# The last stage of a two-layer decoder: three results of a token side by side, read by half batches, one batch added by TensorE

## The chip, the cores and the metric

The kernel runs on one core of one Trainium2 chip. The metric is the device time of one execution in microseconds (us); three runs of the kernel before gave 1203.73, 1205.29 and 1206.92 us, a median of 1205.29. Everything below about where time goes comes from one further execution that was recorded by the hardware profiler.

## The reference, cut to what matters

The network has two layers, each an attention to a context and then a mixture of experts, with residual sums. Only the last mixture matters here: 2048 tokens of 256 numbers, 15 experts of which each token uses 3, and a shared expert that every token uses.

```python
def _L1_ffn_ref(x, gate_w, fc1_w, fc1_b, geglu_mult, fc2_w, fc2_b, s_fc1_w, ...):
    ...
    scores = jax.nn.softmax(xt @ gate_w.T, axis=-1)
    topk_w, topk_idx = jax.lax.top_k(scores, TOPK)              # TOPK = 3 of E = 15
    topk_w = topk_w / (jnp.sum(topk_w, axis=-1, keepdims=True) + 1e-20)
    ...
    a = jax.nn.gelu(g, approximate=False) * xh * geglu_mult[:, None, :]
    yexp = jnp.einsum('etf,edf->etd', a, fc2_w) + fc2_b[:, None, :]
    y = jnp.einsum('etd,te->td', yexp, comb)
    ...
    ys = as_ @ s_fc2_w.T + s_fc2_b
    return (y + ys).reshape(s, b, d)
...
x = x + _L1_ffn_ref(_layernorm(x, axis=-1), ...)
```

## The kernel before, in words

The 2048 tokens are 4 batches of 512. A batch lies in SBUF as one tile `x[b]` of 128 partitions x 4 x 256 numbers (token `k * 128 + p` of the batch in partition `p`, place `k`), 4 KB in each partition. `x[b]` holds the running residual sum all through the kernel and is written to the output at the end.

In the last mixture each token is copied three times, once for each expert that it chose, into a DRAM table ordered by expert (`xs`). With a copy go its weight and the row of the result table `y1` (3 x 2048 rows of 1 KB, in DRAM) into which its result shall be put. This row number is made once by `numbers` (L508): `token1` at L525 gives choice `k` of token `t` the row `k * 2048 + t`, so a batch's results lie in three places of 512 rows each.

The routed experts run by pairs of 128-row tiles in `pipeline` (L469, called near the end of the kernel): `fetch1` loads rows and weights, `turn1` transposes, `hidden1` makes the hidden values (TensorE, ScalarE, VectorE), and `output1` multiplies by the second weights, scales on ScalarE (L1366) and scatters 128 rows to `y1` by an indirect DMA from GpSimd (L1368). These scatters are collected in the list `adds`. Some of the pairs run only if the number of pairs calls for it.

The shared expert has two halves of 256 hidden numbers. `shared_expert(b, new)` (L1179) is a generator: for each half it makes two hidden tiles (L1188 on TensorE, L1194 on ScalarE, and on VectorE the gate in L1174 and L1177), giving way twice for each tile; then for each of the batch's four token tiles it sums four products in PSUM (L1203) and adds the sum to `x[b]` on VectorE (L1207). For batches 0 to 2 all of it is done before the routed experts. For batch 3, `last`, only the first half's hidden tiles are made ahead (four steps of the generator); the rest is left for the end, where it keeps TensorE in work while the scatters land.

The tail, after the pipeline, is this:

- `last` is run to its end (L1405).
- For each batch, in the order 0 to 3, and for each choice `k`, 512 rows of `y1` are read into a tile `yr1` (L1411, by SP's queue, 4 pieces of 1 KB for each partition) and added to `x[b]` in one VectorE instruction of 128x1024 (L1413). The tag `yr1` has 3 buffers. Every read waits for all scatters in `adds`.
- After a batch's three additions `x[b]` is written to the output (L1414), 512 KB in one DMA.

Here the order of the instructions on the engines is chosen by a scheduler. In the rest of the last mixture it is the order of the program's text (`tc.manual_schedule`). In the order that the scheduler chose for the tail, VectorE takes the additions of batch 0 and the first of batch 1 in turn with the two remaining gates of `last`; the four L1207 additions stand after batch 1's second addition. On SP the reads of batch 0 and the first two of batch 1 come first, and an output follows when its additions are done, with the next reads behind it.

Of the kernel before, what the change touches and what calls it, by code (L numbers as in the profile page):

```python
# [12 lines left out]
F32 = mybir.dt.float32  # L13
# [3 lines left out]
ALU = mybir.AluOpType  # L17
AX = mybir.AxisListType
ENG = mybir.EngineType
# [3 lines left out]
P = 128  # L23
B, S, D = 4, 512, 256
T = B * S
NT = T // P
TB = S // P
# [16 lines left out]
PAIR = 2 * P  # L44
# [17 lines left out]
E1, K1, F1 = 15, 3, 256  # L62
E1S = E1 + 2
FC = F1 // P
# [11 lines left out]
def decoder_kernel(ctx: ExitStack, tc: tile.TileContext, a: dict, out: bass.AP):  # L76
    nc = tc.nc
# [5 lines left out]
    def after(ins, earlier, reason):  # L83
        for e in earlier:
            tc.add_manual_dep(
                ins, e.name,
                mybir.DependencyInfo(mybir.DependencyClass.Sync, mybir.DependencyReason.DATA),
                reason=reason,
            )


    x = [const.tile([P, TB, D], F32, name=f"x{b}") for b in range(B)]
# [37 lines left out]
    ident = const.tile([P, P], F32, name="ident")  # L130
# [2 lines left out]
    make_upper_triangular(nc, upper, 1.0, diag=False)  # L133
    ones = const.tile([P, P], F32, name="ones")
    nc.gpsimd.memset(ones, 1.0)


    slots = dram.tile([SLOTS + E0 * T, ROW], F32, name="slots")
    y0 = dram.tile([K0 * T, D], F32, name="y0")
    xs = dram.tile([E1 * T + 2 * PAIR, ROW], F32, name="xs")  # L140
    y1 = dram.tile([K1 * T, D], F32, name="y1")
# [366 lines left out]
    def numbers():  # L508


        def ramp(name, shape, pattern, base=0):
            t = const.tile([P, *shape], F32, name=name)
            nc.gpsimd.iota(t, pattern=pattern, base=base, channel_multiplier=0, allow_small_or_imprecise_dtypes=True)
            return t

        named = ramp("named", (E1,), [[1, E1]])
        slot0 = ramp("slot0", (E0,), [[REGION0, E0]])
        drop0 = ramp("drop0", (E0,), [[T - REGION0, E0]], SLOTS)  # L520
        token0 = const.tile([P, NT, K0], I32, name="token0")
        nc.gpsimd.iota(token0, pattern=[[P, NT], [T, K0]], base=0, channel_multiplier=1)
        slot1 = ramp("slot1", (E1,), [[T, E1]])
        token1 = const.tile([P, NT, K1], I32, name="token1")
        nc.gpsimd.iota(token1, pattern=[[P, NT], [T, K1]], base=0, channel_multiplier=1)  # L525

        def choices(t, n, k):
            return t[:, :n].unsqueeze(1).unsqueeze(1).to_broadcast([P, TB, k, n])

        def tiles(t, n):  # L530
            return t.unsqueeze(1).to_broadcast([P, TB, n])

        index = const.tile([P, 1], F32, name="index")
        nc.gpsimd.iota(index, pattern=[[0, 1]], base=0, channel_multiplier=1, allow_small_or_imprecise_dtypes=True)
        twice = const.tile([P, 1], F32, name="twice")
        nc.gpsimd.iota(twice, pattern=[[0, 1]], base=0, channel_multiplier=2, allow_small_or_imprecise_dtypes=True)
        some0 = ramp("some0", (TILES0,), [[P, TILES0]])
        full0 = const.tile([P, len(FULL0)], F32, name="full0")  # L540
        for i, v in enumerate(FULL0):
            nc.gpsimd.memset(full0[:, i : i + 1], float(v))
        base0 = ramp("base0", (E0,), [[TILES0, E0]], -E0 * TILES0)
        some1 = ramp("some1", (PAIRS1 - 1,), [[PAIR, PAIRS1 - 1]], PAIR)
        base1 = ramp("base1", (E1,), [[PAIRS1, E1]], 1 - E1 * PAIRS1)
        earlier = const.tile([P, E1, E1], F32, name="earlier")
        nc.gpsimd.memset(earlier, 1.0)
        nc.gpsimd.affine_select(
            out=earlier, in_=earlier, compare_op=ALU.is_gt, fill=0.0,
            base=0, pattern=[[1, E1], [-1, E1]], channel_multiplier=0,  # L550
        )
        ffn0.number(choices(named, E0, K0), tiles(slot0, E0), token0, base0)
        ffn1.number(choices(named, E1, K1), tiles(slot1, E1), token1, base1)
        ffn0.drop, ffn0.some, ffn0.full, ffn1.some = tiles(drop0, E0), some0, full0, some1
        return index, named, earlier, twice
# [381 lines left out]
    def begin0(b):  # L937
        if b == 0:
            lists.extend(numbers())
        return iter(())  # L940
# [164 lines left out]
    with ExitStack() as first:  # L1105
# [5 lines left out]
        new = dict(  # L1111
            pt=lambda: ps_t.tile([P, DC, P], F32, name="prt", tag="prt"),
            pg=lambda: ps_h.tile([P, PAIR], F32, name="pg", tag="pg"),
            pu=lambda: ps_h.tile([P, PAIR], F32, name="pu", tag="pu"),
            py=lambda: ps_y.tile([P, D], F32, name="py", tag="py"),
            rT=lambda: mw.tile([P, DC, P], F32, name="rT0", tag="rT0"),
            hT=lambda: mw.tile([P, NF // 2, PAIR], F32, name="hT", tag="hT"),
            sg=lambda: mw.tile([P, PAIR], F32, name="sg", tag="sg"),
            ysb=lambda: mw.tile([P, D], F32, name="ysb", tag="ysb", bufs=6),
# [52 lines left out]
    def gate(o, pv, b1, f, gl):  # L1172

        nc.vector.tensor_scalar(  # L1174
            o, pv, b1[:, f : f + 1], b1[:, 2 * FC + f : 2 * FC + f + 1], ALU.add, ALU.mult
        )
        nc.vector.tensor_tensor(o, o, gl, ALU.mult)  # L1177

    def shared_expert(b, new):  # L1179

        aTs = []
        for w1, w2, b1 in both:
            aT = new["aT"]()
            for f in range(FC):
                pg, pv = new["p"](), new["p"]()
                for ph, col in ((pg, F1 + f * P), (pv, f * P)):
                    for c in range(DC):
                        nc.tensor.matmul(  # L1188
                            ph, w1[:, c, col : col + P], ffn1.xT[b][:, c, :],
                            start=(c == 0), stop=(c == DC - 1),  # L1190
                        )
                    if ph is pg:
                        gl = new["gl"]()
                        nc.scalar.activation(gl, pg, AF.Gelu, bias=b1[:, FC + f : FC + f + 1])  # L1194
                        yield PEP
                gate(aT[f], pv, b1, f, gl)
                yield PEP
            aTs.append((aT, w2))
        for k in range(TB):
            py = new["p"]()[:, :D]  # L1200
            for i, (aT, w2) in enumerate(aTs):
                for f in range(FC):
                    nc.tensor.matmul(  # L1203
                        py, aT[f][:, k * P : (k + 1) * P], w2[:, f, :],
                        start=(i == 0 and f == 0), stop=(i == 1 and f == FC - 1),
                    )
            nc.vector.tensor_tensor(x[b][:, k, :], py, x[b][:, k, :], ALU.add)  # L1207
            yield PEP

# [88 lines left out]
    mp = m1.enter_context(tc.tile_pool(name="m1p", bufs=1))  # L1298
# [54 lines left out]
    adds = []  # L1353

    def output1(p):
# [24 lines left out]
    new = dict(  # L1380
        p=lambda: ps1.tile([P, S], F32, name="p", tag=next(turns)),
        gl=lambda: mp.tile([P, S], F32, name="gl", tag="gl", bufs=2),
        aT=lambda: [mp.tile([P, S], F32, name="aTs", tag="aTs", bufs=4) for _ in range(FC)],
    )
    turns = itertools.cycle(("pg", "pv", "py"))

    with tc.manual_schedule(engines={ENG.PE, ENG.DVE, ENG.Activation, ENG.SP}):
        for p in range(3):
            fetch1(p)
        for b in more:  # L1390
            for step in (shared_expert, biases) if b < B - 1 else (biases,):
                for _ in step(b, new):
                    pass
        last = shared_expert(B - 1, new)
        for _ in range(4):
            next(last)

# [4 lines left out]
    )  # L1402


    for _ in last:  # L1405
        pass
    for b in range(B):
        for k in range(K1):
            yr = mp.tile([P, TB, D], F32, name="yr1", tag="yr1", bufs=3)
            r = k * T + b * S  # L1410
            read = nc.sync.dma_start(yr, y1[r : r + S, :].rearrange("(k p) d -> p k d", p=P))  # L1411
            after(read.ins, adds, "all results")
            nc.vector.tensor_tensor(x[b], x[b], yr, ALU.add)  # L1413
        nc.sync.dma_start(out[b], x[b])  # L1414
    m1.close()


# [101 lines left out]
```

## Time and profile before

| | |
|---|---|
| median of three runs | 1205.29 us (1203.73 to 1206.92) |
| the profiled execution | 1215.69 us |
| its span | 1214.0 us |
| TensorE busy in the span | 1149.4 us (95%) |
| VectorE, ScalarE, GpSimd busy | 620.4, 459.5, 186.5 us |
| mean granted TensorE clock | 0.955 |
| from 1179.0 us to the end: TensorE, VectorE busy of 35.0 us | 10.36, 18.32 us |
| the same stretch: mean granted clock, DMA share, rate | 0.67, 0.73, 240 GB/s |
| from 1000 to 1160 us: TensorE busy | 158.42 of 160.00 us |

The span runs from the first to the last event of the recorded execution; the profiled execution's own time is 1.69 us longer. The profile lists for each instruction its engine, the line of the kernel, the tiles that it writes and reads, its start and its duration, and, in brackets, how long the engine was idle before it and what ended this idle time. PE is TensorE, DVE is VectorE, ACT is ScalarE, POOL is GpSimd, SP the engine that issues most DMAs. The granted clock is the share of full speed that TensorE was given.

### The profile page before, as it was taken

Reading aid. Unit: us, or ns where it says so; the run is one execution under the profiler, and the core shown is the slowest. Engines: PE = TensorE matmul, PEld = TensorE weight load, DVE = VectorE, ACT = ScalarE, POOL = GpSimd, SP = SyncE. Lnnn points to the kernel's source line nnn. Section 1 sums busy time; section 2 is a strip of 40 time slices with the busy share of each in tenths; the row PEclk is TensorE's granted clock in tenths of the full one; section 3 lists DMA queues with packets and bytes.
Section 4 is the critical chain, followed back from the end, with each engine's and each line's share of the span. In section 5 each row is a group of like instructions: output and inputs, shape, how many; then the busy total and the mean of one; then the engine's idle time right before and its main releaser. Section 6 shows DMA issues by size and latency. Waiting matters only on the chain.

```text
span 1214.0 us, 18265 instructions
## 1 busy us (share of the span) xinstructions
PE 1149.4 (95%) x6582; PEld 738.3 (61%) x6582; DVE 620.4 (51%) x1591; ACT 459.5 (38%) x877; POOL 186.5 (15%) x274
## 2 busy tenths in 40 slices
PE   6999997999999999999999999999999999999982
PEld 3334432788999999997433333433336558888862
DVE  6677773531111111114768688867636435444426
ACT  3365464421222222223266576575653102333320
POOL 2000112042000000002000000211322402333330
PEclk7899998999999999999699999999989989999996
DMA  8999107227788888863101000001100135777737
GB/s 321 406 403 403 69 27 264 75 92 292 302 306 326 316 312 305 317 253 106 35 1 36 1 1 1 27 27 36 44 25 28 53 114 160 218 236 214 226 122 244
DMA packets 64405, 204.73 MB, mean 169 GB/s; under 512 B 9502, under 2 KB 31922, under 8 KB 57392
## 3 DMA queue, kind: packets, MB, share of 16 engines
q1 hardware_dynamic: 56144, 182.93, 42.3%
q0 software_dynamic: 8160, 20.52, 4.6%
q8 instruction: 55, 0.90, 0.3%
q14 instruction: 46, 0.38, 0.1%
HBM read 138.57 MB, written 66.70 MB: 169 GB/s over the span
## 4 chain that ended last, share of the span: by engine, by line
PE 44%; DMA 5%; DVE 4%; issue 1%; ACT 0%; POOL 0%; SPq 0%; DVEq 0%; POOLq 0%
PE sc L696 10%; PE av L735 5%; PE shared L1188 4%; PE pg L1307 3%; PE pv L1307 3%; PE pyp L1361 3%; PE sct L720 3%; DMA y<-ysb,rows 2%; DMA yr<-y 2%; PE pp L673 2%; DVE negmax L701 2%; PE shared L1203 1%; PE po L792 1%; PE pa L645 1%; PE pa L673 1%
## 5 line engine op out<-in xcount | busy, mean ns | idle before, releaser
L701 DVE TENSOR_REDUCE negmax<-sc 128x1 f32<-128x512 f32 x384 | 245.6, 683 | 67.8 <-PE sct L720 59.2
L725 ACT ACTIVATE es<-sct 128x512 f32<-128x512 f32 x384 | 208.5, 596 | 155.2 <-PE sct L720 143.6
L696 PE MATMUL sc<-kT,qT 32*128 32x512 f32 x768 | 255.5, 680 | 5.2 <-DVE negmax L701 2.8
L720 PE MATMUL sct<-qa,kT 32*128 32x512 f32 x768 | 254.3, 660 | 1.7 <-DVE qa L711 1.7
L696 PEld LDWEIGHTS sc<-kT,qT 32*128 32x128 f32 x768 | 82.6, 194 | 103.8 <-DVE negmax L701 59.8
L1015 DVE TENSOR_TENSOR hT<-pu,sg 128x256 f32<-128x256 f32 x96 | 40.8, 425 | 136.5 <-PE pu L1006 131.6
L735 PE MATMUL av<-es,v 128*32 128x512 f32 x768 | 107.2, 619 | 0.1
L1006 PE MATMUL pg<-rT,w 128*128 128x128 f32 x768 | 101.5, 275 | 0.1
L1006 PE MATMUL pu<-rT,w 128*128 128x128 f32 x768 | 101.4, 275 | 0.0
L720 PEld LDWEIGHTS sct<-qa,kT 32*128 32x128 f32 x768 | 78.9, 188 | 26.6 <-issue 16.7
L1006 PEld LDWEIGHTS pg<-rT,w 128*128 128x128 f32 x768 | 93.5, 192 | 0.4 <-issue 0.3
L1006 PEld LDWEIGHTS pu<-rT,w 128*128 128x128 f32 x768 | 93.5, 192 | 0.0
L1024 PE MATMUL py<-w,hT 128*128 128x256 f32 x384 | 86.7, 379 | 0.0
L1368 POOL DMA_INDIRECT y<-ysb,rows x60 | 59.0, 984 | 155.1 <-ACT ysb L1366 143.5
L1024 PEld LDWEIGHTS py<-w,hT 128*128 128x128 f32 x384 | 71.2, 190 | 8.7
L1011 ACT ACTIVATE sg<-pg 128x256 f32<-128x256 f32 x96 | 36.8, 383 | 101.5 <-PE pg L1006 100.5
L378 POOL COPY rows<-weight 128x2 f32<-128x2 f32 (+1 forms) x28 | 4.2, 205 | 434.5 <-DVE weight L341 258.6
L735 PEld LDWEIGHTS av<-es,v 128*32 128x32 f32 x768 | 16.0, 109 | 76.7 <-issue 70.6
L1307 PE MATMUL pg<-rTp,wp 128*128 128x256 f32 x240 | 61.8, 380 | 0.6 <-DVE rTp L1345 0.6
L1307 PE MATMUL pv<-rTp,wp 128*128 128x256 f32 x240 | 61.6, 379 | 0.0
L1030 POOL DMA_INDIRECT y<-ysb,rows x24 | 23.6, 982 | 238.7 <-ACT ysb L1028 236.3
L1174 DVE TENSOR_SCALAR aTp<-pv,wp 128x256 f32<-128x256 f32 x60 | 32.6, 544 | 51.4 <-PE pv L1307 48.3
(257 smaller groups left out, 1490.3 us busy)
## 6 DMA issues: line engine op xcount, KB each, us to landing
w<-in_W12T_dram SPq DMA_DIRECT2D x27, 2048.0 KB
xs<-empty SPq DMA_DIRECT2D x61, 516.0 KB
w<-in_W3T_dram SPq DMA_DIRECT2D x27, 1024.0 KB
wp<-in_w1p_dram SPq DMA_DIRECT2D x30, 515.0 KB
yr<-y SPq DMA_DIRECT2D x20, 512.0 KB
rows<-xs SPq DMA_DIRECT2D x30, 258.0 KB
wp<-in_fc2T_dram SPq DMA_DIRECT2D x30, 256.0 KB
slots<-empty SPq DMA_DIRECT2D x11, 516.0 KB
```

The lines of the kernel that those rows point to most:

```text
L696: nc.tensor.matmul(sc, q[u][32 * j : 32 * j + 32, qt * P : (qt + 1) * P], k[u][32 * j : 32 * j + 32, :], start=True, stop=True,)
L701: nc.vector.tensor_reduce(heads[:, qt, j, HELP[s] : HELP[s] + 1], sc, AX.X, ALU.max, negate=True)
L720: nc.tensor.matmul(sc, k[u][32 * j : 32 * j + 32, kt * P : (kt + 1) * P], qa[u][32 * j : 32 * j + 32, :], start=True, stop=True,)
L725: nc.scalar.activation(t, sc, AF.Exp, scale=p["scale"])
L735: nc.tensor.matmul(av[b, g][32 * j : 32 * j + 32, :], vs[b % NV][:, kt, h : h + 32], es[u, kt, j], start=(first and kt == 0), stop=(last a ...
L1006: nc.tensor.matmul(ph[:, i * n : (i + 1) * n], w[:, c, col + i * P : col + (i + 1) * P], rT[:, c, :], start=(c == 0), stop=(c == DC - 1),)
L1011: nc.scalar.activation(sg, pg, AF.Silu)
L1015: nc.vector.tensor_tensor(h, pu, sg, ALU.mult)
L1024: nc.tensor.matmul(py, hT[f][:, i * P : (i + 1) * P], w[:, f, :], start=(f == 0), stop=(f == NF - 1))
L1188: nc.tensor.matmul(ph, w1[:, c, col : col + P], ffn1.xT[b][:, c, :], start=(c == 0), stop=(c == DC - 1),)
L1307: nc.tensor.matmul(ph[:, :n], w1[:, c, col : col + P], rhs[:, c, :], start=(c == 0), stop=(c == DC - 1),)
L1368: ins = nc.gpsimd.indirect_dma_start(out=y1, out_offset=bass.IndirectOffsetOnAxis(ap=rows[:, i, D : D + 1].bitcast(I32), axis=0), in_=ysb[ ...
```

## The change

The row of a result becomes `3 * t + k`, so that a token's three results lie side by side, 3 KB together. The tail reads them by half batches (256 tokens, 786,432 bytes, 2 pieces of 3 KB for each partition), 8 reads in all, each into a buffer of its own (`bufs=2 * B`). The order of the tail on TensorE, VectorE, ScalarE and SP is given by the program's text. All reads are issued first: batch 0, batch 3, then batches 1 and 2. Then `last` takes the four steps of its second half. Then the batches follow in the same order: batches 0, 1 and 2 by half batches, with three VectorE additions of 128x512 and a store of 256 KB for each half; batch 3 by finishing `last`, in which TensorE adds a token tile's three results to the sum of the shared expert in PSUM, by products with the identity matrix, and VectorE adds this sum to `x[3]`. Batch 3 is stored in one DMA of 512 KB.

On VectorE this order is: the two gates, batch 0's six additions, batch 3's four, batch 1's six, batch 2's six. On TensorE each of the four token tiles of batch 3 has seven instructions in a row: four products of the shared expert and three of the identity. On SP the eight reads stand ahead of all seven stores.

```diff
@@ numbers @@
-        nc.gpsimd.iota(token1, pattern=[[P, NT], [T, K1]], base=0, channel_multiplier=1)
+        nc.gpsimd.iota(token1, pattern=[[P * K1, NT], [1, K1]], base=0, channel_multiplier=K1)
@@ shared_expert @@
-    def shared_expert(b, new):
+    def shared_expert(b, new, results=None):
...
-                        start=(i == 0 and f == 0), stop=(i == 1 and f == FC - 1),
+                        start=(i == 0 and f == 0), stop=(results is None and i == 1 and f == FC - 1),
                     )
+            if results:
+                for c in range(K1):
+                    nc.tensor.matmul(py, ident, results(k, c), start=False, stop=(c == K1 - 1))
             nc.vector.tensor_tensor(x[b][:, k, :], py, x[b][:, k, :], ALU.add)
             yield PEP
@@ decoder_kernel @@
-        last = shared_expert(B - 1, new)
+        found = {}
+        last = shared_expert(B - 1, new, lambda k, c: found[B - 1, k // 2][:, k % 2, c * D : (c + 1) * D])
         for _ in range(4):
             next(last)
...
-    for _ in last:
-        pass
-    for b in range(B):
-        for k in range(K1):
-            yr = mp.tile([P, TB, D], F32, name="yr1", tag="yr1", bufs=3)
-            r = k * T + b * S
-            read = nc.sync.dma_start(yr, y1[r : r + S, :].rearrange("(k p) d -> p k d", p=P))
-            after(read.ins, adds, "all results")
-            nc.vector.tensor_tensor(x[b], x[b], yr, ALU.add)
-        nc.sync.dma_start(out[b], x[b])
+    with tc.manual_schedule(engines={ENG.PE, ENG.DVE, ENG.Activation, ENG.SP}):
+        for b in (0, B - 1, *range(1, B - 1)):
+            for h in range(2):
+                found[b, h] = mp.tile([P, 2, K1 * D], F32, name="yr1", tag="yr1", bufs=2 * B)
+                r = (b * S + h * PAIR) * K1
+                src = y1[r : r + PAIR * K1, :].rearrange("(k p c) d -> p k (c d)", p=P, c=K1)
+                after(nc.sync.dma_start(found[b, h], src).ins, adds, "all results")
+        for _ in range(4):
+            next(last)
+        for b in (0, B - 1, *range(1, B - 1)):
+            if b == B - 1:
+                for _ in last:
+                    pass
+                nc.sync.dma_start(out[b], x[b])
+                continue
+            for h in range(2):
+                xs = x[b][:, 2 * h : 2 * h + 2, :]
+                for c in range(K1):
+                    nc.vector.tensor_tensor(xs, xs, found[b, h][:, :, c * D : (c + 1) * D], ALU.add)
+                nc.sync.dma_start(out[b][:, 2 * h : 2 * h + 2, :], xs)
```

## The prediction

> **What bounds the kernel now.** I read the page's chain of waits first. Its shares say that TensorE sets most of the span, but the change touches only what comes after the routed experts, so the shares say little here. I then asked for the timeline of the last 60 us.
>
> ```profile
> 1174.82 0.98 POOL L1368 DMA_INDIRECT y<-ysb,rows  x1 [0.30 <-issue]
> ...
> 1179.06 8.45 SPq L1411 DMA_DIRECT2D yr<-y  x5
> ...
> 1180.45 1.03 PE L1203 MATMUL p<-ctxT,aTs 128*128 128x256 f32 x4
> ...
> 1184.05 1.22 DVE L1413 TENSOR_TENSOR x<-x,yr 128x1024 f32<-128x1024 f32 x1 [14.50 <-DMA yr<-y]
> 1185.19 0.80 DVE L1174 TENSOR_SCALAR aTs<-p,ctxT 128x512 f32<-128x512 f32 x1
> ...
> 1187.79 7.88 PE L1203 MATMUL p<-ctxT,aTs 128*128 128x256 f32 x28 [6.31 <-DVE aTs L1177]
> ...
> 1197.89 1.23 DVE L1413 TENSOR_TENSOR x<-x,yr 128x1024 f32<-128x1024 f32 x1 [0.23 <-DMA yr<-y]
> 1201.93 1.23 DVE L1413 TENSOR_TENSOR x<-x,yr 128x1024 f32<-128x1024 f32 x1 [2.82 <-DMA yr<-y]
> ...
> 1208.42 1.23 DVE L1413 TENSOR_TENSOR x<-x,yr 128x1024 f32<-128x1024 f32 x1 [2.37 <-DMA yr<-y]
> 1209.68 0.35 SPq L1414 DMA_DIRECT2D out_dram<-x  x1
> ```
>
> The last scatter of results is issued at 1174.82 and has landed by 1179.06, when SP may read them. What follows is a tail of 35 us. VectorE adds each read as it lands and is short of reads: the last waits of 2.82 and 2.37 us end with a landing. The chain of waits agrees: from 1179.5 on it is four stretches of "DMA yr<-y" of 6.81, 5.53, 5.22 and 4.74 us with an addition after each. A read cannot be issued before one of three buffers is free. The windows show that this, and not the DMA engines, holds the reads back.
>
> ```profile
> 1182.50:1183.50 1.00, 0.00 (x0) 0.00 (x0) 0.00 (x0) 0.00 (x0) 0.00 (x0) 1.00 1.06 374
> ...
> 1185.50:1186.00 0.50, 0.00 (x0) 0.00 (x0) 0.50 (x2) 0.00 (x0) 0.00 (x0) 0.50 0.18 61
> 1186.00:1190.50 4.50, 2.71 (x6) 2.19 (x7) 4.50 (x5) 0.00 (x0) 0.00 (x0) 0.50 0.73 235
> ...
> 1191.00:1191.50 0.50, 0.50 (x4) 0.45 (x3) 0.32 (x1) 0.00 (x0) 0.00 (x0) 1.00 1.06 248
> ```
>
> The last three columns are TensorE's granted clock, the DMA engines' share and GB/s. While the first three reads (1.57 MB) move, the rate is 374 GB/s; when all three buffers are full it falls to 61. The clock column matters too: TensorE idled 6.31 us, its clock fell to 0.50, and it was back at 1.00 by 1191.0, 3.2 us after work began again at 1187.79.
>
> **The reads.** The scatter's rows change place in DRAM but stay 1 KB rows, 60 scatters as before (984 ns each on POOL); I cost that at nothing, and the end at 1179.06 stays. There are now 8 reads of 786,432 B in place of 12 of 524,288 B: the same 6.29 MB, each with a buffer of its own, so SP issues them one after another at 0.36 to 0.50 us each, all before any output. A row is now 3 KB. Rows of 1 KB moved at 373 GB/s (above); the first loads, rows of 4 KB, at 406 to 418:
>
> ```profile
> 9.00:11.00 2.00, 1.69 (x5) 0.61 (x3) 0.55 (x3) 1.58 (x3) 0.00 (x0) 1.00 1.02 406
> ```
>
> I take 406, the nearer row, and keep 373 as the other bound. One read is then 0.786/406 = 1.94 us (2.11). The first read of now was issued at 1179.06 and released VectorE at 1184.05: 4.99 us, of which its bytes at 373 are 1.41 and 3.58 is fixed. So the first new read lands at 1179.06 + 3.58 + 1.94 = 1184.6 and the following ones 1.94 us apart: batch 0 at 1184.6 and 1186.5, batch 3 at 1188.5 and 1190.4, batches 1 and 2 at 1192.3, 1194.3, 1196.2 and 1198.2. Now the last one lands at 1208.4. By the reads alone some 10 us are gained.
>
> The Trainium skill has a rule against cutting transfers up: in "DMA: Bandwidth & Descriptors", section "Measured (HBM→SBUF, 128 partitions, SWDGE, issued from GpSimd)", one is to batch to at least 1 MiB, and "Anatomy of one DMA" gives about 2.0 us + bytes/436 GB/s for each. If each read paid that alone, eight would take 8 x 3.8 = 30.4 us and the last would land at 1209.5, with the end 1 to 2 us later than now. The windows above speak against it: queued reads ran without a gap at 374 GB/s.
>
> **Batch 3 on TensorE.** VectorE now makes the gates (L1174, L1177) without an addition ahead of them: the last matmul before them ends at 1180.45, and 0.80 + 0.11 + 0.69 us later, at about 1182.1, all four hidden halves are there (now 1191.3). TensorE runs the fourth product of token tile 0 and then waits in order for batch 3's first read at 1188.5; behind it stand 3 additions by identity and 7 instructions of tile 1 (4 products, 3 additions), then 14 for tiles 2 and 3, 24 in all, 12 of them new. At full clock one is 0.216 us apart from the next (L1361's 16 in 3.62 us); at half clock 0.43. The idle from 1182.5 to 1188.5 is as long as now's, so I take half clock for 3.2 us (7.4 instructions) and full for 16.6: 1188.5 + 3.2 + 16.6 x 0.216 = 1195.3. Bounds: full clock throughout, 1190.4 + 14 x 0.216 = 1193.4; half throughout, 1188.5 + 24 x 0.43 = 1198.8.
>
> "TensorE: Matmul & The Clock Gate", section "Part 1: The HAM clock gate (the "warmup" mystery)", says that the window is free-running; by it the return could come up to 6.8 us after the restart, TensorE's end at 1197.0 and the sum 1.7 us later than mine. The one return in this tail (3.2 us) does not tell.
>
> **The additions on VectorE.** In the given order they are: batch 0 (6), batch 3's four L1207 additions, batch 1 (6), batch 2 (6). Each of the 18 is 128x512:
>
> ```profile
> L1245 DVE TENSOR_TENSOR x<-x,yr x16: 681/685/693, 562.1 to 725.4; 128x512 f32<-128x512 f32 x16
> ...
> L1413 DVE TENSOR_TENSOR x<-x,yr x12: 1215/1225/1226, 1184.1 to 1208.4; 128x1024 f32<-128x1024 f32 x12
> ```
>
> Two independent ones take 1.29 us together, so one follows after 0.605. Three in a row now write the same slice, and each waits for the one before: the nearest row is L1177 behind L1174, which starts 0.11 us after its end, so 0.795 from start to start. Bounds: 0.605 (no such gap), and 0.685 + 0.23 (the gap before the addition at 1197.89). Batch 0 is added by 1186.5 + 2.3 = 1188.8 or so, under the reads. Then VectorE waits with TensorE for batch 3, and batches 1 and 2 stand behind it although three of their four reads have landed. That is the new bound: 1195.3 + 0.3 (L1207 pipelined) = 1195.6 for the first of twelve; three halves of 0.605 + 2 x 0.795 = 2.195, then 2 x 0.795 + 0.685: 1195.6 + 6.6 + 2.3 = 1204.5. Without the 0.11 gaps it is 8 x 0.19 = 1.5 earlier, with 0.23 it is 1.0 later.
>
> **The outputs.** 2.1 MB in seven stores, all but the last hidden: they queue behind the reads and go out from about 1197 while VectorE adds. If that cover were gone, 1.84 MB at 406 would cost 4.5 us. Now the last addition ends at 1209.65 and the span at 1214.0: 4.35 us for 512 KB. The last store is 256 KB, 0.65 less at 406: 3.70. End: 1204.5 + 3.7 = 1208.2.
>
> **Sum.** 1214.0 - 1208.2 = 5.8 us less. The profiled execution took 1215.69 us, 1.69 around its span, and 10.4 more than the median of 1205.29; I take the difference over unchanged: 1205.3 - 5.8 = 1199.5.
>
> **Rivals.**
> - *TensorE stays cold, or the reads are slow* (no change that can be told). At half clock throughout batch 3 is done 3.5 us later: 1203.0. Reads at the tail's present mean of 249 GB/s (3.16 us each) would bring batch 3's first read to 1192.1, 3.6 us later: 1203.1. For it: the half clock from 1186.0 to 1190.5, and a TensorE that waits between bursts. Against it: the 1.00 at 1191.0, and 374 GB/s wherever reads were queued.
> - *VectorE and the clock are kinder*: no gaps (1.5) and full clock (1.9): 1196.1. For it: the clock stood at 1.00 until 1184. Against it: the one idle of this length in the tail, 6.31 us, cost the clock.
> - *Slower: the reads land together.* Eight reads share the same DMA engines; if these divided their time among them, none would land before about 1198.2. TensorE would end at 1198.2 + 6.8 = 1205.0, the additions at 1214.2, the span at 1217.9: +3.9, 1209.2. Past batch 3's first read everything moves one for one, so it decides from a landing at 1194.3 instead of 1188.5. Against it: now's first read released VectorE at 1184.05 with two more behind it, and the third landed by 1186.86: in turn.
> - *The change does nothing* would need the reads to be bound by the engines already; 61 GB/s at 1185.5 speaks against it, and I give it no chance of its own.
>
> **How the numbers follow.** Forecast 0.62, no change to be told 0.18, kinder 0.12, slower 0.08. A measurement here can tell 0.3%, 3.6 us. The forecast's own range, 1197.5 to 1202, lies nearly all beyond it (1201.7): faster 0.62 + 0.12 less 0.03 = 0.71, same 0.18 + 0.03 = 0.21, slower 0.08. The range runs from the kind bounds, 1196.1, to the cold clock with the dear gap (1203.0 + 1.0) and some of the slow reads: 1204.5. Beyond are the slower case and a little of each side.
>
> **What would show it.** Eight reads issued by about 1183 to 1186 and landing some 2 us apart; the rate near 400 GB/s without a hole until 1196; batch 3's additions on TensorE starting near 1188.5 at clock 0.50 and ending near 1195; then twelve additions of 0.685 us without a wait for DMA, and the last store some 3.7 us before the end. If batch 1's additions wait for DMA, or batch 3's last product ends after 1200, I am wrong.

## The result, and the profile after

The time hardly moved. Twenty runs of the changed kernel have a median of 1205.14 us (1200.70 to 1211.97), twenty of the kernel before one of 1206.53 (1203.48 to 1212.40); the ratio is 0.999, with a 95% interval from 0.9978 to 1.0003. That is no change that can be told. The forecast was 5.8 us less.

The two profiled spans mislead: 1214.0 us before, 1200.7 after, 13.3 apart. What the change touches is the tail, from SP's issue of the first read of `y1` to the end of the span: 1214.0 - 1179.06 = 34.9 us before, 1200.7 - 1167.21 = 33.5 after. The other 11.9 us lie ahead of the first read, where the programs differ in little but the rows that the scatters write. That stretch varies from one execution to the next: the kernel before, with only its buffers changed (below), issued its first read at 1170.02, 9.0 us ahead of 1179.06, and the changed kernel in a second execution at 1172.26, 5.1 us behind 1167.21. The profiled execution of the kernel before, 1215.69 us, was also longer than all of its twenty runs. So the tail is compared in what follows, and the second execution of the changed kernel (below) shows how far it can be trusted. The tail lost 1.4 us, as much as the medians; neither loss is shown to be more than chance, since the interval of the ratio includes 1 and the tail of the kernel before was recorded once.

The timeline of the tail, changed kernel, all engines (start, duration, engine, line; in brackets the idle time before and what ended it):

```profile
1167.21 5.40 SPq L1417 DMA_DIRECT2D yr<-y  x8
...
1171.90 4.20 DVE L1429 TENSOR_TENSOR x<-x,yr 128x512 f32<-128x512 f32 x6 [1.78 <-DMA yr<-y]
...
1175.85 2.93 PE L1210 MATMUL p<-yr,ident 128*128 128x256 f32 x6 [4.97 <-DMA yr<-y]
...
1178.57 2.41 PE L1204 MATMUL p<-ctxT,aTs 128*128 128x256 f32 x8
...
1186.87 1.46 PE L1210 MATMUL p<-yr,ident 128*128 128x256 f32 x6
1188.37 0.42 DVE L1211 TENSOR_TENSOR x<-p,x 128x256 f32<-128x256 f32 x1 [2.60 <-PE p L1210]
1188.71 8.30 DVE L1429 TENSOR_TENSOR x<-x,yr 128x512 f32<-128x512 f32 x12
...
1190.87 6.50 SPq L1430 DMA_DIRECT2D out_dram<-x  x4
```

The reads do what was forecast: eight in a row, batch 0 added from 1171.90 on, and after the change no addition of L1429 waits for DMA beyond the first. But TensorE works on batch 3 from 1175.85 to 1188.33, 12.5 us, and VectorE waits for batch 3's sums until 1188.37, with all of batches 1 and 2 behind them in its queue. The windows of the same stretch (clock, DMA share and GB/s are the last three columns) show that the data had long been there:

```profile
1173.00:1175.00 2.00, 0.00 (x0) 0.00 (x0) 1.93 (x4) 0.00 (x0) 0.00 (x0) 0.50 1.04 413
...
1183.00:1185.00 2.00, 2.00 (x11) 1.76 (x10) 0.00 (x0) 0.00 (x0) 0.00 (x0) 1.00 1.03 391
1185.00:1187.00 2.00, 2.00 (x11) 1.75 (x10) 0.42 (x1) 0.00 (x0) 0.00 (x0) 1.00 0.46 177
1187.00:1189.00 2.00, 1.33 (x7) 0.82 (x5) 0.63 (x2) 0.00 (x0) 0.00 (x0) 1.00 0.03 11
```

The DMA engines run near 400 GB/s until about 1186 and then stand idle, because the next stores wait for VectorE. Before the change VectorE waited for reads; now it waits for TensorE. The stall did not go away; another engine causes it.

### The profile page after: what moved, and what is told of

It is laid out like the page before. It is cut to its first block, busy times and chain, and to the rows that moved or that the text cites. A ratio compares the mean times of both kernels' runs of the same rounds, so it can differ in the third digit from the quotient of the medians.

```text
span 1200.7 us, 18308 instructions
## 1 busy us (share of the span) xinstructions
PE 1142.4 (95%) x6606; PEld 740.0 (62%) x6606; DVE 618.6 (52%) x1597; ACT 459.8 (38%) x877; POOL 186.5 (16%) x274
## 4 chain that ended last, share of the span: by engine, by line
PE 47%; DVE 4%; DMA 2%; ACT 0%; issue 0%; SPq 0%; DVEq 0%
PE sc L697 10%; PE av L736 5%; PE pg L1311 4%; PE pv L1311 4%; PE pyp L1365 4%; PE shared L1189 4%; PE sct L721 2%; PE pp L674 2%; DVE negmax L702 2%; PE shared L1204 1%; DMA y<-ysb,rows 1%; PE po L793 1%; PE pa L646 1%; PE pa L674 1%; PE ptp L1345 1%; PE p L1189 1%
## 5 line engine op out<-in xcount | busy, mean ns | idle before, releaser
L697 PE MATMUL sc<-kT,qT 32*128 32x512 f32 x768 | 251.4, 657 | 5.2 <-DVE negmax L702 3.1
L721 PE MATMUL sct<-qa,kT 32*128 32x512 f32 x768 | 250.9, 650 | 2.6 <-DVE qa L712 2.6
L721 PEld LDWEIGHTS sct<-qa,kT 32*128 32x128 f32 x768 | 78.5, 186 | 25.7 <-issue 15.4
L1175 DVE TENSOR_SCALAR aTp<-pv,wp 128x256 f32<-128x256 f32 x60 | 32.6, 544 | 51.4 <-PE pv L1311 51.4
```

The source lines that it names most:

```text
L697: nc.tensor.matmul(sc, q[u][32 * j : 32 * j + 32, qt * P : (qt + 1) * P], k[u][32 * j : 32 * j + 32, :], start=True, stop=True,)
L721: nc.tensor.matmul(sc, k[u][32 * j : 32 * j + 32, kt * P : (kt + 1) * P], qa[u][32 * j : 32 * j + 32, :], start=True, stop=True,)
```

## The experiments

All of them are judged by the tail. Those with a ratio were timed against the kernel before on the same chip; the others were executed once, with the profile.

**Sums last.** One line of the tail is changed: the order in which the batches are added. Batch 3's four sums now stand last on VectorE, and its store last on SP.

```diff
-        for b in (0, B - 1, *range(1, B - 1)):
+        for b in range(B):
             if b == B - 1:
                 for _ in last:
```

> Everything of the changed kernel is kept but one line: batch 3's four sums stand behind the additions of batches 1 and 2 on VectorE, and its store behind theirs on SP; the reads keep their order. The tail, from the issue of the first read of y1 to the end of the span, is 34.9 us in the kernel before and 33.5 in the changed one. Queue theory: VectorE waits for TensorE's 12.5 us of batch 3 with the additions of batches 1 and 2 behind it. Then these run as their reads land, the last of them ends about 20.6 us after the first issue, the sums of batch 3 by 22, its 512 KB store 4.35 later: a tail of 26 to 27 us, a ratio to before of about 0.993. Transfer theory: the landings or the stores set the end anyway, tail 32 us or more. VectorE theory: the sum of its own additions is the bound, tail about 33.

Measured: 1199.03 us (7 runs) against 1207.63 (19 runs), ratio 0.9936 (0.9914 to 0.9958); tail 1201.3 - 1173.89 = 27.4 us. VectorE in this kernel's timeline:

```profile
1178.63 4.20 DVE L1429 TENSOR_TENSOR x<-x,yr 128x512 f32<-128x512 f32 x6 [1.81 <-DMA yr<-y]
1186.47 2.14 DVE L1429 TENSOR_TENSOR x<-x,yr 128x512 f32<-128x512 f32 x3 [3.64 <-DMA yr<-y]
1189.31 6.34 DVE L1429 TENSOR_TENSOR x<-x,yr 128x512 f32<-128x512 f32 x9 [0.70 <-DMA yr<-y]
1195.56 1.41 DVE L1211 TENSOR_TENSOR x<-p,x 128x256 f32<-128x256 f32 x4
```

Batches 1 and 2 are added while TensorE works, with waits for their reads alone, and the four sums run together at the end. Same work, same reads, 6 us less: the place of four additions in VectorE's queue is what held the gain back. (The store that moved with them is not: in the changed kernel SP issues it at 1188.82, and the next store, at 1190.87, waits for VectorE.)

**No identity.** Batch 3 is added by VectorE like the others; the order 0, 3, 1, 2 stays.

```diff
-        last = shared_expert(B - 1, new, lambda k, c: found[B - 1, k // 2][:, k % 2, c * D : (c + 1) * D])
+        last = shared_expert(B - 1, new)
...
             if b == B - 1:
                 for _ in last:
                     pass
-                nc.sync.dma_start(out[b], x[b])
-                continue
```

> Batch 3's results are added by VectorE, like the other batches', and not by TensorE: the 12 products with the identity go, 6 additions of 128x512 come (24 in all), batch 3 is stored by halves; reads, buffers and the order 0, 3, 1, 2 stay. Queue theory: what costs is that TensorE's products of batch 3 wait for a read and are slow after the wait; without the identity they end some 9 us after the first issue, VectorE then adds without a wait, 24 x 0.69 + 4 x 0.35 = 18 us from the first landing at 4.7: about 23, and the last store 3.7: a tail of 26 to 27 us, ratio about 0.993, in spite of more work for VectorE. VectorE theory: six additions more are 4.2 us more, tail about 37.5. Transfer theory: 32 or more.

Measured: 1199.16 us (7 runs), ratio 0.9942 (0.9922 to 0.9962); tail 1196.4 - 1169.72 = 26.7 us. TensorE's products and VectorE's additions in its timeline:

```profile
1173.10 5.90 PE L1204 MATMUL p<-ctxT,aTs 128*128 128x256 f32 x26 [0.40 <-DVE aTs L1178]
```

```profile
1174.24 4.20 DVE L1427 TENSOR_TENSOR x<-x,yr 128x512 f32<-128x512 f32 x6 [1.20 <-DMA yr<-y]
1178.36 1.41 DVE L1211 TENSOR_TENSOR x<-p,x 128x256 f32<-128x256 f32 x4
1179.69 12.41 DVE L1427 TENSOR_TENSOR x<-x,yr 128x512 f32<-128x512 f32 x18
```

Without the identity TensorE waits for no read, is done by 1179.0, and VectorE adds without a gap to 1192.1. Six additions more on the engine that sets the end, and the kernel is faster than the changed one: taking them off VectorE was no gain as long as VectorE then waited for their replacement.

**Only the buffers.** The kernel before, with 12 buffers in place of 3.

```diff
-            yr = mp.tile([P, TB, D], F32, name="yr1", tag="yr1", bufs=3)
+            yr = mp.tile([P, TB, D], F32, name="yr1", tag="yr1", bufs=B * K1)
```

> The kernel before with one edit: 12 buffers for the reads in place of 3. Rows, whole batches, VectorE's additions and the scheduler's order stay. If the three buffers alone held the reads back, as my prediction said, all reads land 1.42 us apart, the last 20.5 us after the first issue, and the tail is about 28.5 us. If the order on SP does it as well (stores, which wait for VectorE, stand ahead of reads 7, 9 and 12), the reads still come in groups and the tail is 32 to 34 us, nearly as before (34.9).

Measured: 1207.41 us (12 runs), ratio 1.0005 (0.9988 to 1.0021); tail 1203.6 - 1170.02 = 33.6 us. SP's queue:

```profile
1170.02 4.61 SPq L1411 DMA_DIRECT2D yr<-y  x6
1179.26 0.35 SPq L1414 DMA_DIRECT2D out_dram<-x  x1
1179.65 1.48 SPq L1411 DMA_DIRECT2D yr<-y  x2
1186.77 0.35 SPq L1414 DMA_DIRECT2D out_dram<-x  x1
1187.17 2.13 SPq L1411 DMA_DIRECT2D yr<-y  x3
```

After the sixth read SP stands for 4.6 us at the store of batch 0, which waits for VectorE, with free buffers and reads behind it. (With 12 buffers the scheduler places six reads ahead of this store; it was five.) So the three buffers were only one of two holds on the reads; the scheduler's order on SP was the other, and the buffers alone are worth nothing that can be told: this tail is 1.3 us shorter than the one recorded before, but the interval of the times goes from 1.4 us less to 2.5 more.

**Three buffers in the changed kernel** (`bufs=2 * B` becomes `bufs=3`).

> The changed kernel with 3 buffers for the reads in place of 8. If in the changed order VectorE's wait for TensorE sets the end, the reads of batches 1 and 2 may come late at little cost: from the release of the buffers the last read lands at about 28.5 us after the first issue, and the tail is about 34.3 (33.5 with 8). If buffers are what counts, as my prediction had it, the tail goes past 37.

Measured in one execution: tail 1210.7 - 1174.65 = 36.1 us, between the two expectations (34.3, and past 37) and nearer to the second.

```profile
1195.64 6.25 DVE L1429 TENSOR_TENSOR x<-x,yr 128x512 f32<-128x512 f32 x9
1203.94 2.14 DVE L1429 TENSOR_TENSOR x<-x,yr 128x512 f32<-128x512 f32 x3 [2.06 <-DMA yr<-y]
```

VectorE waited 2.06 us for the last read, after it had waited for TensorE as before. So in the given order the buffers are worth 2.4 to 2.6 us (against the 33.7 and 33.5 of the changed kernel), though alone, in the scheduler's order, they brought nothing that can be told.

**A warm TensorE.** Twelve products that nobody reads fill its wait.

```diff
             if results:
+                if k == 0:
+                    pw = new["p"]()[:, :D]
+                    for _ in range(12):
+                        nc.tensor.matmul(pw, ident, w2[:, 0, :], start=True, stop=True)
                 for c in range(K1):
```

> The changed kernel with 12 products of 128x256 more, into a PSUM tile that nobody reads, between batch 3's first four products and its first product with the identity: they fill TensorE's wait of 5 us for the read, so that its clock stays up. If the half clock after the wait is what made batch 3 slow, its 24 products take about 10.4 us in place of 12.5 and the tail is about 31.5 us. If the number of products is the cost and the clock little, the tail stays within 0.5 us of 33.5.

Measured in one execution: tail 1206.1 - 1173.42 = 32.7 us, between the two expectations. TensorE in its timeline:

```profile
1177.42 5.34 PE L1212 MATMUL p<-ctxT,ident 128*128 128x256 f32 x24
1183.04 1.56 PE L1214 MATMUL p<-yr,ident 128*128 128x256 f32 x6 [0.28 <-DMA yr<-y]
1184.43 1.89 PE L1204 MATMUL p<-ctxT,aTs 128*128 128x256 f32 x8
...
1192.22 1.46 PE L1214 MATMUL p<-yr,ident 128*128 128x256 f32 x6
```

Batch 3 takes 1193.68 - 1183.04 = 10.6 us at full clock, so of the 12.5 us the cold clock is 1.8. The other 10.6 are the number of products. But the first read of batch 3 landed 9.6 us after the first issue, where the changed kernel has 8.6, and about half of the 1.8 was lost again. The same kernel was executed once more for that:

> The kernel with the 12 filling products once more: in the first look batch 3's first read landed 9.6 us after the first issue, in two looks of the changed kernel 8.6. If the filling products hold the reads back, it lands at 9.3 or later again and the tail is again within 1 us of the changed kernel's (33.5 and 33.7); if that was chance, at 8.5 to 9.0, and the tail is 31.5 to 32.

```profile
1185.51 1.56 PE L1214 MATMUL p<-yr,ident 128*128 128x256 f32 x6 [0.78 <-DMA yr<-y]
```

It landed at 9.6 again (1185.51 - 1175.89), and the tail was 1208.6 - 1175.89 = 32.7 again. That the landing is later with the filling products is shown twice; why, is open. Landings also came about a microsecond later than an even 1.97 us apart in two kernels without them (the sixth read of sums last, at 15.4; the fourth of the kernel by landing, at 11.6), so it need not be the products.

**Rows apart.** The results in their old rows, read in 12 reads of whole batches into 12 buffers, all else as changed.

```diff
-        nc.gpsimd.iota(token1, pattern=[[P * K1, NT], [1, K1]], base=0, channel_multiplier=K1)
+        nc.gpsimd.iota(token1, pattern=[[P, NT], [T, K1]], base=0, channel_multiplier=1)
...
+            for c in range(K1):
+                found[b, c] = mp.tile([P, TB, D], F32, name="yr1", tag="yr1", bufs=K1 * B)
+                r = c * T + b * S
+                src = y1[r : r + S, :].rearrange("(k p) d -> p k d", p=P)
```

> The changed kernel with the results in their old rows (a token's three results 2048 rows apart), so read by whole batches and choices in rows of 1 KB, 12 reads into 12 buffers, otherwise in the given order. Batch 3 can then be begun by TensorE only when its third read, the sixth of all, has landed: 4.7 + 5 x 1.42 = 11.8 us after the first issue in place of 8.6. Queue theory: all behind it moves by these 3 us, tail 36 to 37, longer than before the change (34.9). If the size and order of the reads count for nothing, 33.5.

Measured in one execution: tail 1203.6 - 1167.34 = 36.3 us, as the queue theory had it. TensorE's first products with the identity come one by one behind the reads:

```profile
1176.90 1.22 PE L1210 MATMUL p<-yr,ident 128*128 128x256 f32 x2 [5.57 <-DMA yr<-y]
1178.41 1.22 PE L1210 MATMUL p<-yr,ident 128*128 128x256 f32 x2 [0.29 <-DMA yr<-y]
1179.92 1.22 PE L1210 MATMUL p<-yr,ident 128*128 128x256 f32 x2 [0.29 <-DMA yr<-y]
```

The third is there 12.6 us after the first issue (11.8 were expected), not 8.6. Side by side and by halves is thus worth 2.8 us of the tail in this order; without it the tail would be 1.3 us longer than the one before the change.

**By landing.** Reads half by half in the order 3, 0, 3, 0, 1, 1, 2, 2; VectorE takes each half as it lands, the sums where they are ready.

```diff
-        for b in (0, B - 1, *range(1, B - 1)):
-            for h in range(2):
+        halves = [(B - 1, 0), (0, 0), (B - 1, 1), (0, 1)] + [(b, h) for b in range(1, B - 1) for h in range(2)]
+        for b, h in halves:
...
+        add(0, 0)
+        next(last)
+        next(last)
+        store(B - 1, 0)
+        add(0, 1)
+        add(1, 0)
+        next(last)
+        add(1, 1)
+        next(last)
+        store(B - 1, 1)
+        add(2, 0)
+        add(2, 1)
```

> The changed kernel with another order: reads half by half as batch 3, 0, 3, 0, 1, 1, 2, 2; VectorE takes each half in the order in which its reads land and TensorE's sums where they are ready, batch 3 is stored by halves. Queue theory: TensorE waits about 1 us for the first read and keeps its clock (24 products in 10.4 us, done some 15 us after the first issue), VectorE has 18 x 0.69 + 4 x 0.35 = 14 us of work from the landing of the second read at 6.7 on and ends at 21 to 22; with the last store of 3.7 us the tail is 25 to 26 us, about a microsecond less than in the two kernels before (27.4 with the sums last, 26.7 without the identity). If stores and reads share a bound that these two had reached, it stays at 26.5 or more.

Measured: 1200.12 us (7 runs) against 1208.32 (12 runs), ratio 0.9929 (0.9904 to 0.9953); tail 1199.0 - 1172.45 = 26.6 us. That is above the 25 to 26 of the queue theory and at the 26.5 where the other expectation begins; the microsecond that was to be gained on the two kernels above did not come.

```profile
1178.96 2.15 DVE L1427 TENSOR_TENSOR x<-x,yr 128x512 f32<-128x512 f32 x3 [3.54 <-DMA yr<-y]
1181.03 0.42 DVE L1211 TENSOR_TENSOR x<-p,x 128x256 f32<-128x256 f32 x1
1181.64 0.42 DVE L1211 TENSOR_TENSOR x<-p,x 128x256 f32<-128x256 f32 x1 [0.20 <-PE p L1210]
1184.00 4.20 DVE L1427 TENSOR_TENSOR x<-x,yr 128x512 f32<-128x512 f32 x6 [1.93 <-DMA yr<-y]
```

VectorE now waits for TensorE only 0.20 us, and batch 3 took 10.6 us at full clock, but the fourth read (before 1184.00) came a microsecond late. From then on VectorE worked without a wait until 1195.02 (its last row there starts at 1190.83 and takes 4.19 us), so neither reads nor stores held it any more, and the late read accounts for the microsecond; whether a bound that reads and stores share made it late is not shown. The three kernels that free VectorE's queue have ratios that overlap; no one of them is shown to be the best. All beat the kernel before, and by their ratios (0.9962 at most, against 0.9978 at least) the changed kernel too.

**The changed kernel again.**

> The changed kernel once more, to see how far the tail of one look is from that of another: 33.5 us within 0.7 if the tail does not share the spread of the whole runs (1200.7 to 1212.0 us), some 5 us apart if it does.

The tail was 1206.0 - 1172.26 = 33.7 us, 0.2 from the first execution, while the span was 5.3 longer. In these two the tail does not share the spread of whole runs.

## Why the prediction was wrong, point by point

**The bound before** was half read. That the reads were held back and not the DMA engines was right, and so was the waiting VectorE. That "A read cannot be issued before one of three buffers is free" was the hold is not enough: with 12 buffers SP stood at its stores. The trace of before had it: from 1179 us on SP waited 7.7 us at stores (L1414) that had reads behind them, for VectorE's additions, and 11.2 us at reads (L1411).

**The reads** were right. 406 GB/s was taken for rows of 3 KB; the windows show 391 to 418. Batch 3's first read, the third of all, landed 8.6 us after the first issue; 9.4 were forecast. The first had landed at 4.69, so two more took 1.97 each, and the fixed part was 2.7 us in place of 3.58. The last of them is not seen alone, but nothing waited for it.

**Batch 3 on TensorE** is the step that failed: "24 in all, 12 of them new. At full clock one is 0.216 us apart from the next (L1361's 16 in 3.62 us)". The 24 are instructions of the program, but the 16 in that row are records of the profile, and here a product of 32-bit numbers leaves two of them. The profile of before said so; its group and the one of after:

```profile
L1203 PE MATMUL p<-ctxT,aTs x32: 377/379/795, 1180.5 to 1195.3; 128*128 128x256 f32 x32
```

```profile
L1210 PE MATMUL p<-yr,ident x24: 377/379/794, 1175.8 to 1187.9; 128*128 128x256 f32 x24
```

L1203 is 4 token tiles x 4 products = 16, and has 32 records; L1210 is 12 and has 24. A product is 0.43 us at full clock, not 0.216, and about twice that at half clock (the first six records took 2.72 us, from 1175.85 to 1178.57). The 24 instructions are 48 records. By the forecast's own way, half clock for 3.2 us (7.4 records) and full for the other 40.6, they take 3.2 + 40.6 x 0.216 = 12.0 us in place of 6.8; measured 12.5. With that one number right the sum would have been 5.2 us longer, a gain of 0.6, and the time 1204.7 for a measured 1205.14. The prediction's own sign of being wrong came with it: batch 3's last product was not to end after 1200, 20.9 us after the first issue, and ended 21.1 after it (1188.33 - 1167.21).

The Trainium skill could have caught it: "FP8 and Floating Point Precision", section "TensorE Precision Notes", says that true FP32 takes 4 passes through the array. By "TensorE: Matmul & The Clock Gate", section "Wait — 56ns, not 53.3ns?", matmuls of N columns start N / 2.4 GHz and about 2.5 ns apart at full clock; four passes of 256 columns are then 0.44 us, an estimate. This trace agrees: 0.43 for a product, two records of 0.216.

**The clock** was right in its size: it was back 3.7 us after the restart, with 3.2 forecast; 1.8 of the 12.5 us hang on it.

```profile
1179.50:1180.00 0.50, 0.50 (x4) 0.45 (x3) 0.00 (x0) 0.00 (x0) 0.00 (x0) 0.89 1.11 414
```

The clock column is 0.89 here, so the half clock ended near 1179.6. The 3.2 us are not a constant: in the second execution of the changed kernel the clock was 0.77 on the mean from 1184.26 to 1186.26, so it was back about 4.3 us after the restart at 1180.88, and batch 3 took 12.75 us.

**The additions** were slightly too dear. Twelve took 8.30 us for 8.9. The gap of 0.11 us behind a dependent instruction, taken from L1174 and L1177, is not there: in the chain of waits of the changed kernel they follow within 0.02 us.

```profile
1191.46 0.02 issue
1191.48 0.70 DVE x L1429
1192.18 0.02 issue
```

Between the two gates the 0.11 us is still there (L1175 ends at 1169.33, L1178 starts at 1169.44); it was the wrong neighbour to take. The 0.23 us of the upper bound stand in their row as a wait for a read. **The last store** was right: 1200.7 less the additions' end at 1197.01 is 3.7 us.

Together: 5.7 longer on TensorE, 0.8 less for the reads, 0.6 less for the additions, 0.1 more between, is 4.4 of the 5.8 us that had been forecast, and leaves 1.4. That the reads and the additions gave back 1.4 us of the error is luck: neither has to do with it. The new bound, VectorE behind TensorE, had been named, with batches 1 and 2 standing behind batch 3; it was its price that was wrong.

**The rivals.** The time fell into the case of no change, but not by its reasons: TensorE did not stay cold and the reads were not slow. The case of reads that land together did not come.

## What to carry to other kernels

Before a count of instructions is multiplied by a row's duration, the row's own count is divided by the program's count for a line that both know; here 32 to 16 would have saved the forecast. Where a scheduler's order is replaced by one written out, each engine's queue is read for what stands behind a wait: an instruction that waits for another engine belongs behind all that is ready without it. And buffers that seem to hold transfers back are worth what the queue that issues the transfers lets them be worth: alone nothing that can be told here, in the given order some 2.5 us in one execution.

## What the runs showed of the hardware that was not expected

- Dependent VectorE additions of 128x512 follow one another almost as closely as their length allows: in the changed kernel they start 0.72 us apart (1191.48 and 1192.20), 0.70 of work and 0.02 of gap, against 0.605 for independent ones.
- Queued reads of 3 KB rows moved at 391 to 418 GB/s (windows of 2 us in the changed kernel), those of 1 KB rows at 336 to 358 in the kernel with rows apart.
- Landings of queued reads are not even: about 1.97 us apart for 786 KB in the changed kernel, but in three others (a warm TensorE, sums last, by landing) one came about a microsecond later; by landing the rate stayed at 398 GB/s meanwhile. The cause is open.
